# Layer 3's loop: the Exp of a step in two parts, and the values of a step gathered one step ahead

## The chip, the core and the metric

The kernel runs on one core of a Trainium2 chip. The core has five engines that work in parallel, each on its own queue of instructions: TensorE (PE, matrix products into PSUM), VectorE (DVE), ScalarE (ACT), GpSimd (POOL) and SyncE (SP). DMA engines move data between HBM and the on-chip memory SBUF; any of several engines can issue a DMA. The metric is the device time of one execution in microseconds; the number that counts is the median of several runs.

## The reference

Four graph layers run one after the other on a graph of N = 2708 nodes with 128 features and a dense 0/1 adjacency matrix A. Only the fourth (layer 3) is touched by the change:

```python
XW = X @ W
s_col = XW @ a[0, :f];  s_row = XW @ a[0, f:]
Z1 = leaky_relu(s_row[:, None] + s_col[None, :], negative_slope=0.01)
den = exp(Z1)
num = A @ den
att = where(num != 0, den / where(num != 0, num, 1.0), 0.0)
H = A @ (att @ XW)
```

Computed as written, `A @ den` would be a product of two N x N matrices. The kernel uses that `den[r, c]` depends on the two scores alone, and that the leaky relu has two straight pieces: for the columns sorted by score, most of a column of `num` is a running sum over the rows in order of their scores, plus a remainder over a few rows close to the place where the piece changes.

## The kernel before, in words

Layers 0 to 2 are streaming products of the adjacency with the features. Layer 3 then has four stages:

1. Ranks. Every node gets its rank by row score and a slot by column score (lines 679 to 1067), which gives tables: `xw_i` (which 128 nodes form step s), `row_i` (which 124 rows of the transposed adjacency a row set q needs) and `pre_i` (which 4 rows of running sums).
2. Running sums (`sums`, line 818), written to HBM as `pre_d`.
3. The loop over NE = 22 steps of 128 columns each (lines 1183 to 1224). This is where the change is.
4. The last product A @ (att @ XW) (line 1287), with the adjacency streamed in once more by SP's DMAs, into buffers that the loop has freed.

**One step s of the loop.** A step has two row sets, q = 2s and 2s + 1. A row set is a 128 x 2708 tile: 124 gathered adjacency rows and 4 rows of running sums. There are four buffers for them, `hT`, `row_b`, `hs`, `yT` (`regained[q % 4]`).

- `fetch_xw(s)` (line 666, issued by POOL): an indirect DMA that gathers the 128 rows of XW that belong to step s, the *values*, into one of four buffers `xw_s[s % 4]`.
- `fetch_step(s + 2)` (line 1156, POOL): four indirect DMAs, in this order: the rows of set 2s + 4 (`gather_rows`), the running sums of set 2s + 3 (`carry`), the rows of set 2s + 5, the running sums of set 2s + 4. A `carry` writes into the same buffer as its `gather_rows` and waits until those rows have landed.
- VectorE: `xw` times a factor (line 1189), the shifted relu into a tile `e` of 128 x 2708 (line 1193, two buffers for `e`), four small operations that split the next weights into a high and a low part (`densities_of`, lines 1175 and 1176).
- TensorE: `num` in six blocks of 512 columns, four matmuls each (line 1206), through two PSUM banks.
- ScalarE: Ln of each block (line 1211) as it is done, which also frees the bank.
- VectorE: three subtractions `e - ln` (line 1214), of 1536, 1024 and 148 columns.
- `halved(2s + 2)` on VectorE and `halved(2s + 3)` on ScalarE (line 1168): the conversion of the row sets of step s + 1 to the type that the matmuls of line 1206 read.
- ScalarE: Exp over the whole of `e` (line 1220): att for these 128 columns.
- TensorE: `spread_values(s - 1)` (line 1147): twelve matmul instructions (line 1150) that multiply the step's values by the `e` of the step before and add to six accumulators. They come after the products of step s, and free the `e` buffer that the relu of step s + 1 writes.

**What sets the order.** A planner places the instructions on each engine's queue and adds the semaphores. Nearly all of the loop is wrapped in `keep_in_program_order`, which holds these instructions of an engine in the order of the source. `fetch_xw` is not wrapped. The branch taken with this input is `exact`: all conditions on `exact` are true. All issues of POOL carry line 647 in the profile, since they go through the helper `gather`; they are told apart by their tiles.

Of the kernel before, what the change touches and what calls it, by code (L numbers as in the profile page):

```python
# [13 lines left out]
AF = mybir.ActivationFunctionType  # L14
# [5 lines left out]
def kernel(  # L20
# [19 lines left out]
    nc = tc.nc  # L40
# [16 lines left out]
    CUT = 3 * 512  # L57
# [35 lines left out]
    def bank():  # L93
        return ps.tile([P, 512], F32, tag="bank", name="bank")
# [69 lines left out]
    NE = T  # L164
# [321 lines left out]
    def rest(exact, stack3):  # L486
# [159 lines left out]
        def gather(out, src, idx):  # L646
            return nc.gpsimd.indirect_dma_start(  # L647
                out=out,
                out_offset=None,
                in_=src,  # L650
                in_offset=bass.IndirectOffsetOnAxis(ap=idx, axis=0),
            )
# [7 lines left out]
        def gather_rows(a, s):  # L660

            m = gather(a, adj_t[:, :], row_i[:, s : s + 1])
            tc.keep_in_program_order(m)
            return a

        def fetch_xw(s):
            gather(xw_s[s % 4], xw_d[:, :], xw_i[:, s : s + 1])
# [465 lines left out]
        def carry(s):  # L1133
            a = regained[s % 4]
            m = gather(a[SUMS[0] : SUMS[-1] + 1 : SUMS[1] - SUMS[0], :], pre_d[:, :], pre_i[: P - CH, s : s + 1])
            tc.keep_in_program_order(m)
            return a
# [9 lines left out]
        def spread_values(s):  # L1147
            xw, e = done.pop(s)
            for b, (lo, hi) in enumerate(E0):
                m = nc.tensor.matmul(accs[b][:, : hi - lo], xw, e[:, lo:hi], start=(s == 0), stop=(s == NE - 1))  # L1150
                tc.keep_in_program_order(m)

        with tc.tile_pool(name="att", bufs=2) as attp:
            terms = {}

            def fetch_step(s):

                for q in (2 * s, 2 * s + 1):
                    if q < NS:
                        gather_rows(regained[q % 4], q)  # L1160
                    if q <= NS:
                        rows_of[q - 1] = carry(q - 1)

            def halved(q):

                a = rows_of.pop(q)
                r = steps.tile([P, N], F32R, tag="rows", name="rows")
                m = nc.scalar.copy(r, a) if q % 2 else nc.vector.tensor_copy(r, a)  # L1168
                tc.keep_in_program_order(m)
                return r  # L1170

            def densities_of(q):
                d_hi = attp.tile([P, P], F32R, tag=f"d_hi{q % 2}", name="d_hi")
                d_lo = attp.tile([P, P], F32R, tag=f"d_lo{q % 2}", name="d_lo")
                tc.keep_in_program_order(nc.vector.tensor_copy(d_hi, dmat[:, q, :]))
                tc.keep_in_program_order(nc.vector.tensor_sub(d_lo, dmat[:, q, :], d_hi))
                return [d_hi, d_lo]

            nc.scalar.preload_act_table_set("natural_log_exp_and_others")
            if exact:  # L1180
                moving = {q: halved(q) for q in range(2)}
                weights = {q: densities_of(q) for q in range(2)}
            for s in range(NE):
                if s >= 3:
                    fetch_xw(s)
                if exact:
                    fetch_step(s + 2)
                xw = xw_s[s % 4]
                tc.keep_in_program_order(nc.vector.tensor_scalar_mul(xw, xw, c_exp[:, s : s + 1]))  # L1189
                e = attp.tile([P, N], F32, tag="e", name="e")  # L1190
                ln = attp.tile([P, N], F32, tag="ln", name="ln", bufs=1)
                tc.keep_in_program_order(
                    nc.vector.tensor_scalar(e, row_a[:, :N], c_rel[:, s : s + 1], 0.0, ALU.add, ALU.max)
                )
                halves = (2 * s, 2 * s + 1)
                if exact:
                    products = [(d, moving[q]) for q in halves for d in weights[q]]
                    if s + 1 < NE:
                        weights = {q + 2: densities_of(q + 2) for q in halves}
                else:  # L1200
                    products = [(dmat[:, q, :], rows_of.pop(q)) for q in halves]
                beg = 0
                for b, (lo, hi) in enumerate(E0):
                    num = bank()
                    for i, (d, a) in enumerate(products):
                        m = nc.tensor.matmul(  # L1206
                            num[:, : hi - lo], d, a[:, lo:hi], start=(i == 0), stop=(i == len(products) - 1)
                        )
                        tc.keep_in_program_order(m)
                    tc.keep_in_program_order(  # L1210
                        nc.scalar.activation(ln[:, lo:hi], num[:, : hi - lo], AF.Ln, bias=tiny)  # L1211
                    )
                    if b in (2, 4, 5):
                        tc.keep_in_program_order(nc.vector.tensor_sub(e[:, beg:hi], e[:, beg:hi], ln[:, beg:hi]))  # L1214
                        beg = hi
                if not exact:
                    fetch_step(s + 2)
                elif s + 1 < NE:
                    moving = {q + 2: halved(q + 2) for q in halves}
                tc.keep_in_program_order(nc.scalar.activation(e, e, AF.Exp))  # L1220
                done[s] = (xw, e)
                if s:
                    spread_values(s - 1)
            spread_values(NE - 1)
# [65 lines left out]
    with tc.If(some_low > 0) as general:  # L1290
        with ExitStack() as s3:
            rest(False, s3)
    with general.Else():
        with ExitStack() as s3:
            rest(True, s3)
# [32 lines left out]
```

## Time and profile before

| | |
|---|---|
| median of three runs | 851.61 us (849.99 to 853.9) |
| the profiled execution's own time | 853.49 us |
| its span in the profile | 851.7 us |
| busy in the span: PE, DVE, ACT, POOL | 729.7, 583.7, 536.1, 189.2 us |
| mean granted TensorE clock | 0.932 |
| the loop of layer 3 | about 533 to 779 us of the span |
| HBM read | 214.12 MB, 256 GB/s over the span |

Times in the profile are microseconds from the span's start. A line of the list of waits reads: waiting engine, tile and line, what it waited for, then the total, how often, and the longest. A line of the timeline reads: start, duration, engine, line, operation, output <- inputs, and in brackets the idle time of the engine just before it with what ended it. In the timeline `DMA_INDIRECT xw<-xw_d,xw_i` is a step's gather of values, `hT<-in_adj_t_dram,row_i` (or `row_b`, `hs`, `yT`) a gather of rows, and `hT<-pre_d,pre_i` a carry. The duration of such an issue is that of the issue on POOL, not of the transfer. "issue" in a bracket means that the engine waited for nothing that the profile shows.

### The profile page before, as it was taken

The page shows a single profiled execution, that of the slowest core. Times are in us where ns is not written, and L with a number is a line of the kernel's source. Part 1 is how long each engine was busy: PE and PEld are TensorE (multiplying, and loading weights), DVE is VectorE, ACT ScalarE, POOL GpSimd, SP SyncE. Part 2 cuts the span into 40 slices and gives each one's busy share as a digit, 9 for nine tenths or more (in the row PEclk, how much of TensorE's full clock was granted, in tenths as well). Part 3 has the DMA queues.
Part 4 walks back from the last instruction along what each step waited for, and adds up shares of the span by engine and source line. Part 5 has one row for each costly group of instructions (what it writes and reads, how often), then busy time and mean ns, then how long its engine had stood idle before and what let it go on. Part 6 is the DMA issues. An engine that isn't in the chain of part 4 may idle for free.

```text
span 851.7 us, 9005 instructions
## 1 busy us (share of the span) xinstructions
PE 729.7 (86%) x3113; PEld 440.8 (52%) x3113; DVE 583.7 (69%) x1112; ACT 536.1 (63%) x595; POOL 189.2 (22%) x161
## 2 busy tenths in 40 slices
PE   3599999995996979978649785798999989989997
PEld 2333333332775858756216531555555555555785
DVE  5499879786824363447988967776666666655854
ACT  3889999995845473437860026678778777767000
POOL 3000000012201010002000113446666666620010
PEclk9899999997897989988879995899999999999999
DMA  9044444723997989975505985677777776785994
GB/s 339 3 148 180 177 164 182 305 78 148 355 393 284 365 330 395 419 294 208 186 0 184 401 333 210 239 282 272 273 257 287 263 279 255 278 306 229 404 427 139
DMA packets 39476, 218.63 MB, mean 257 GB/s; under 512 B 5108, under 2 KB 13999, under 8 KB 25359
## 3 DMA queue, kind: packets, MB, share of 16 engines
q1 hardware_dynamic: 27704, 150.19, 45.6%
q0 software_dynamic: 8624, 65.76, 21.1%
q10 hardware_dynamic: 3090, 1.99, 0.7%
q8 instruction: 27, 0.44, 0.2%
q14 instruction: 31, 0.25, 0.1%
HBM read 214.12 MB, written 3.79 MB: 256 GB/s over the span
## 4 chain that ended last, share of the span: by engine, by line
PE 14%; DMA 12%; DVE 9%; issue 6%; POOL 6%; ACT 5%; SPq 0%; DVEq 0%; POOLq 0%; ACTq 0%
PE acc L1150 4%; PE bank L1206 4%; DMA hs<-in_adj_t_dram 4%; DMA row_b<-pre_d,pre_i 3%; PE acc L835 2%; DMA row_b<-in_adj_t_dram 2%; ACT rows L1168 2%; POOL hT L647 2%; POOL hs L647 1%; DMA yT<-pre_d,pre_i 1%; PE acc L224 1%; POOL row_b L647 1%; ACT row_a L747 1%; DVE rows L1283 1%; DVE bits L744 1%
## 5 line engine op out<-in xcount | busy, mean ns | idle before, releaser
L1206 PE MATMUL bank<-rows,d_hi 128*128 128x512 f32 (+1 forms) x264 | 106.5, 408 | 24.4 <-ACT ln L1211 12.7
L224 PE MATMUL acc<-rows,h_hi 128*128 128x512 f32 (+1 forms) x264 | 106.5, 408 | 10.3 <-ACT rows L529 6.0
L1150 PE MATMUL acc<-e,xw 128*128 128x512 f32 (+1 forms) x264 | 104.3, 545 | 0.0
L1211 ACT ACTIVATE ln<-bank,tiny 128x512 f32<-128x512 f32 x132 | 79.8, 632 | 33.1 <-PE bank L1206 32.9
L1206 PE MATMUL bank<-rows,d_lo 128*128 128x512 f32 (+1 forms) x264 | 98.7, 385 | 0.0
L224 PE MATMUL acc<-rows,h_lo 128*128 128x512 f32 (+1 forms) x264 | 98.0, 388 | 0.2 <-DVE h_lo L506 0.2
L1214 DVE TENSOR_TENSOR e<-e,ln 128x1536 f32<-128x1536 f32 (+2 forms) x66 | 70.0, 1097 | 15.9 <-ACT ln L1211 15.6
L1206 PEld LDWEIGHTS bank<-rows,d_hi 128*128 128x128 f32 x264 | 51.6, 195 | 53.1 <-ACT ln L1211 31.7
L358 DVE SCALAR_TENSOR_TENSOR tau<-tau,e_hi,a 128x1536 f32<-128x1536 f32 (+1 forms) x44 | 70.5, 1623 | 9.7 <-DMA a<-in_adj_dram 5.6
L1150 PEld LDWEIGHTS acc<-e,xw 128*128 128x128 f32 x264 | 48.4, 190 | 52.6 <-issue 52.6
L355 ACT ACTIVATE tau<-row_a,e_neg,e_lo 128x1536 f32<-128x1536 f32 (+1 forms) x44 | 65.7, 1504 | 3.3 <-PE bank L367 3.2
L224 PEld LDWEIGHTS acc<-rows,h_hi 128*128 128x128 f32 x264 | 52.5, 199 | 24.3 <-ACT rows L529 8.3
L367 PE MATMUL bank<-tau,ones_at 128*32 128x512 f32 (+1 forms) x264 | 51.8, 566 | 8.3 <-DVE tau L358 8.3
L224 PEld LDWEIGHTS acc<-rows,h_lo 128*128 128x128 f32 x264 | 52.6, 200 | 11.8 <-issue 1.9
L1220 ACT ACTIVATE e<-e 128x2708 f32<-128x2708 f32 x22 | 54.1, 2461 | 3.3 <-DVE e L1214 3.3
L224 PE MATMUL acc<-yT,hs 128*128 128x512 f32 x132 | 56.1, 563 | 0.0
L224 PE MATMUL acc<-row_b,hs 128*128 128x512 f32 x132 | 55.3, 557 | 0.0
L1206 PEld LDWEIGHTS bank<-rows,d_lo 128*128 128x128 f32 x264 | 51.6, 195 | 7.0
L224 PE MATMUL acc<-rows,y_hi 128*128 128x512 f32 x132 | 49.8, 384 | 3.8 <-DVE rows L1283 1.9
L224 PE MATMUL acc<-rows,y_lo 128*128 128x512 f32 x132 | 48.4, 382 | 0.0
L529 ACT CAST rows<-dflat 128x1536 fp32r<-128x1536 f32 (+1 forms) x26 | 34.2, 1330 | 20.6 <-DMA dflat<-in_adj_dram 11.2
L1189 DVE TENSOR_SCALAR xw<-xw,c_exp 128x128 f32<-128x128 f32 x22 | 6.4, 290 | 58.2 <-DMA xw<-xw_d,xw_i 58.2
(411 smaller groups left out, 1415.4 us busy)
## 6 DMA issues: line engine op xcount, KB each, us to landing
a<-in_adj_dram SPq DMA_DIRECT2D x21, 1354.0 KB
rows<-in_adj_t_dram SPq DMA_DIRECT2D x16, 1354.0 KB
dflat<-in_adj_t_dram SPq DMA_DIRECT2D x9, 768.0 KB
rows<-in_adj_t_dram SPq DMA_DIRECT2D x9, 768.0 KB
dflat<-in_adj_dram SPq DMA_DIRECT2D x9, 768.0 KB
rows<-in_adj_dram SPq DMA_DIRECT2D x9, 768.0 KB
dflat<-in_adj_t_dram SPq DMA_DIRECT2D x5, 1354.0 KB
hs<-in_adj_t_dram SPq DMA_DIRECT2D x5, 1354.0 KB
```

Source lines behind the costliest of these rows:

```text
L224: nc.tensor.matmul(accs[b][:, : hi - lo], w, moving[:, lo - at : hi - at], start=start and i == 0, stop=stop and i == len(parts) - 1,)
L355: nc.scalar.activation(tau[:, :w], row_a[:, h0:h1], AF.Relu, bias=e_neg[:, t : t + 1], scale=e_lo[:, t : t + 1])
L358: nc.vector.scalar_tensor_tensor(tau[:, :w], tau[:, :w], e_hi[:, t : t + 1], a[:, h0:h1], ALU.add, ALU.mult)
L367: nc.tensor.matmul(den[g : g + 32, : hi - lo], ones_at[:, b // GR, :], tau[:, lo - h0 : hi - h0], start=(t == 0 and b < GR), stop=(t == T ...
L529: m = nc.vector.tensor_copy(r, a) if i % 2 and i > 4 else nc.scalar.copy(r, a)
L647: return nc.gpsimd.indirect_dma_start(out=out, out_offset=None, in_=src, in_offset=bass.IndirectOffsetOnAxis(ap=idx, axis=0),)
L835: m = nc.tensor.matmul(accs[b][64 * h : 64 * h + 2 * NC, : hi - lo], w[:r, t, :], a[:r, lo:hi], start=(t == 0 and i == 0), stop=(t == T - ...
L1150: m = nc.tensor.matmul(accs[b][:, : hi - lo], xw, e[:, lo:hi], start=(s == 0), stop=(s == NE - 1))
L1206: m = nc.tensor.matmul(num[:, : hi - lo], d, a[:, lo:hi], start=(i == 0), stop=(i == len(products) - 1))
L1211: nc.scalar.activation(ln[:, lo:hi], num[:, : hi - lo], AF.Ln, bias=tiny)
L1214: tc.keep_in_program_order(nc.vector.tensor_sub(e[:, beg:hi], e[:, beg:hi], ln[:, beg:hi]))
L1220: tc.keep_in_program_order(nc.scalar.activation(e, e, AF.Exp))
```

## The change

In each step, the values of the next step are gathered in place of the step's own: `fetch_xw(s + 1)` for 3 <= s + 1 < 22, at the same place in the source, ahead of `fetch_step`. The call for step 3's values thus stands in step 2, and the last step makes none. And the Exp is made in two parts: columns 0 to 1535 (`CUT` is 3 * 512, which is also where the first subtraction ends) before the two conversions of the next row sets, and the other 1172 columns after them, where the whole Exp was. The work is the same, with one more ScalarE instruction per step.

```diff
             for s in range(NE):
-                if s >= 3:
-                    fetch_xw(s)
+                if 3 <= s + 1 < NE:
+                    fetch_xw(s + 1)
                 if exact:
                     fetch_step(s + 2)
                 xw = xw_s[s % 4]
...
                         beg = hi
+                tc.keep_in_program_order(nc.scalar.activation(e[:, :CUT], e[:, :CUT], AF.Exp))
                 if not exact:
                     fetch_step(s + 2)
                 elif s + 1 < NE:
                     moving = {q + 2: halved(q + 2) for q in halves}
-                tc.keep_in_program_order(nc.scalar.activation(e, e, AF.Exp))
+                tc.keep_in_program_order(nc.scalar.activation(e[:, CUT:], e[:, CUT:], AF.Exp))
                 done[s] = (xw, e)
```

## The prediction

> **What bounds the kernel now.** I read the waits of 560 to 760 us first: the loop of layer 3 runs from 533 to 779 us, some 10.7 us a step.
>
> ```profile
> DVE xw L1189 <- DMA xw<-xw_d,xw_i: 58.2, 17, 7.7
> POOL hs L647 <- DMA hs<-in_adj_t_dram,row_i: 24.2, 9, 4.0
> POOL hT L647 <- DMA hT<-in_adj_t_dram,row_i: 21.4, 9, 2.8
> PE bank L1206 <- ACT ln L1211: 12.2, 14, 1.2
> ACT rows L1168 <- DMA yT<-pre_d,pre_i: 11.6, 9, 2.0
> ```
>
> The largest wait is the one that the change removes: VectorE waits 3.4 us a step for the values `xw`. But it is no proof of a gain; who sets the pace? GpSimd (POOL) waits for none of the other engines here, only for its own gathers. Its timeline for one step (start, duration; the bracket is the idle time before it):
>
> ```profile
> 640.42 0.95 POOL L647 DMA_INDIRECT xw<-xw_d,xw_i  x1 [0.30 <-issue]
> 641.68 0.93 POOL L647 DMA_INDIRECT hT<-in_adj_t_dram,row_i  x1 [0.30 <-issue]
> 642.92 1.92 POOL L647 DMA_INDIRECT yT<-pre_d,pre_i  x1 [0.30 <-issue]
> 645.14 0.95 POOL L647 DMA_INDIRECT row_b<-in_adj_t_dram,row_i  x1 [0.30 <-issue]
> 648.38 2.24 POOL L647 DMA_INDIRECT hT<-pre_d,pre_i  x1 [2.29 <-DMA hT<-in_adj_t_dram,row_i]
> 650.92 0.95 POOL L647 DMA_INDIRECT xw<-xw_d,xw_i  x1 [0.30 <-issue]
> ```
>
> I call the five V (values), A (first row gather), b (carry for the row before), B (second gather), a (carry into A's row, which waits until A has landed). The ring A, landing, a, V, A closes on itself. Sixteen steps give A 0.94, landing 5.94 (5.52 to 6.28) after its record ends, a 2.30, V 0.95 and two gaps of 0.30: **10.73 us**. V to V from 575.86 to 747.83 is 171.97/16 = 10.75. So POOL paces the loop; PE, stalled 0.5 to 1.2 us a step by a late Ln, needs only 9.92 (its products in the step without a stall: 561.42 to 571.34).
>
> Why is a 2.24 here, and b 1.92, when an undisturbed carry takes 0.90? VectorE's rows of the same step:
>
> ```profile
> 642.91 0.29 DVE L1189 TENSOR_SCALAR xw<-xw,c_exp 128x128 f32<-128x128 f32 x1 [2.89 <-DMA xw<-xw_d,xw_i]
> 643.11 1.62 DVE L1193 TENSOR_SCALAR e<-row_a,c_rel 128x2708 f32<-128x2708 f32 x1
> 648.96 1.56 DVE L1168 CAST rows<-hs 128x2708 fp32r<-128x2708 f32 x1
> ```
>
> b ends at 644.84, 0.11 after the relu (643.11 to 644.73); a at 650.62, 0.10 after the conversion. Through all 95 POOL issues of the loop one rule holds within 0.03 us on average: an issue that begins inside such an operation, or inside a subtraction (L1214), goes on when that ends and takes 0.77 more; one that begins up to about 0.3 us before the relu or the conversion is held to its end plus 0.1; with 0.5 us it gets through.
>
> [...]
>
> **The change, part by part.**
>
> *Exp in two.* ACT's conversions of the two widths show the price: 1.47 us at 1536, 1.15 at 1172, together 2.62 for 2.46, +0.16 a step (3.5 us over 22 steps if uncovered). The cover is ACT's wait for the carried row, 0.4 to 2.0 us a step. The first part can start when the Ln's end, 6.1 us after the products begin; it holds ACT for 1.38 and is done at 7.5; the row comes later than that (below). The next Ln starts after 2.35 + 1.08 instead of 2.35 + 2.36 us from the conversion: 1.28 earlier. That ends PE's stall. Alone it gains little, since POOL paces. The first part adds a wait for the first subtraction, over at 5.7, and the conversion and PE's next products stand behind it; uncovered it would cost them its 1.38 a step.
>
> *Values a step ahead.* The same five issues in the same order; V merely carries the next index, and its buffer was free some 11 us before. VectorE's 3.4 us of waiting disappear, but what follows moves too: today the relu falls 2.7 us after V, harmlessly on b, because it waits for V. Afterwards it starts when PE leaves the buffer `e`, and that is on V and A, in the ring; behind V in POOL's queue stand A, b, B and a, and both conversions wait for these.
>
> The new step, in offsets from c, the start of a: ACT's conversion begins 0.36 later (mean of 17), products at c + 2.86. VectorE's conversion H starts 7.30 after the products (573.22 against 565.91, the step without a stall), so c + 10.16. The relu R starts 5.43 + 4.80 after the products: H + 2.93. An a inside H ends at H + 2.33:
>
> ```profile
> 573.22 1.56 DVE L1168 CAST rows<-hT 128x2708 fp32r<-128x2708 f32 x1
> ```
> ```profile
> 573.85 1.70 POOL L647 DMA_INDIRECT hs<-pre_d,pre_i  x1 [3.99 <-DMA hs<-in_adj_t_dram,row_i]
> 575.86 0.95 POOL L647 DMA_INDIRECT xw<-xw_d,xw_i  x1 [0.30 <-PE acc L1150]
> ```
>
> So V starts at H + 2.64, 0.29 before R[...].
> - V held: it ends at R + 1.72, H + 4.65; A from H + 4.95, through R's small followers to H + 5.85; it lands at H + 11.79.
> - V through: A starts at H + 3.89, inside R, and ends 0.77 after it, H + 5.32; it lands at H + 11.26.
>
> The landing is the next a. With u = c − H, the period is 10.16 + u, and the next u is 1.63 − u (held) or 1.10 − u (through): u swings about a mean of 0.82 or 0.55. The period is **10.98** or **10.71**; scatter of 0.3 us in the landings will give both, and I take 10.85, 0.10 over today's. From A(4) to A(19) are 15 periods: +1.5 (−0.6 to +3.4). The gain at a (2.30 becomes some 1.5) is spent at V or A.
>
> *The start.* In step 0 nothing hides the first part: products of step 1 at 544.9 for 543.96. Step 3 gets a V that it hadn't (the fourth values were fetched before the loop): its A starts near 566.8, in the relu, ends near 568.9 for 566.08 and lands at 574.8 for 573.85; A(4) ends near 579.4 for 578.06: **+1.4** (0 to 2).
>
> *The end.* Step 20's values are issued at 747.83, when the last layer's loads begin, and land 7.3 us later:
>
> ```profile
> 755.13 0.29 DVE L1189 TENSOR_SCALAR xw<-xw,c_exp 128x128 f32<-128x128 f32 x1 [7.70 <-DMA xw<-xw_d,xw_i]
> ```
> ```profile
> 762.54 0.76 PE L1206 MATMUL bank<-rows,d_hi 128*128 128x512 f32 x1 [3.40 <-DVE rows L1168]
> ```
>
> Relu, subtractions and conversion follow late, PE stands idle and then runs its products at a lower clock (0.63 for 0.40 us each), 6.88 us to the next spread. Afterwards those values are there; ACT's conversion (756.40, still late behind the loads) sets the start, 758.9; the products take 5.5. Spread at 764.4 for 769.42: **−5.0** (−3.6 to −5.5). Step 21's values land near 755 and are needed near 758. The last product's loads wait for buffers that this loop frees (from 778.80), so the end moves with the loop.
>
> **Sum:** +1.4 + 1.5 − 5.0 = −2.1. On the profiled execution's 853.49 (span 851.7) that is 851.4; on the runs' median 851.61, 1.9 below the profiled one, it is **849.5**. About 0.5%, 4.3 us, is what a measurement of this kernel can tell from no change.
>
> **Rivals.**
> 1. *POOL gets free.* If a slips past the subtractions, or landings come at 5.5 us, the ring falls below PE's 9.95: 15 × 0.80 = 12 less, and the end's 5: about 836; in part of the steps, 843. For it: POOL issues undisturbed would cost 9.4 a step. Against it: a earlier than H falls into the subtractions, and is held all the same.
> 2. *The relu ahead of V (the slower side).* If R starts a few tenths earlier than H + 2.64, V waits for all of it, ends at R + 2.39, A at R + 3.65: landing at H + 12.25, u's mean 1.05, period 11.21. 15 × 0.46 = 6.9, + 1.4 − 5.0 = +3.3: 854.9; with landings at their slowest, 6.28 (half of the 0.34 counts), or only half of the end's gain, 857.5. It decides from R − V below zero, 0.3 us from my figure; over 0.5% it needs a period of 11.28.
> 3. *The change doesn't do as it says.* `fetch_xw` isn't pinned, and the planner could leave V where it was. Then only the split works: PE's stall goes, a meets less of H, period some 10.4, no gain at the end: 846.5. Against it: V lies in program order in every step from the fourth.
>
> **How the numbers follow.** Forecast 0.50 (its own range 846.5 to 853), rival 1 0.15, rival 2 0.30, rival 3 0.05. Faster by over 0.5% (below 847.3): rival 1, half of rival 3, a fifth of the forecast: 0.27. Slower (above 855.9): half of rival 2 and a fifth of the forecast[...]: 0.25. The rest, 0.48, within. Range 842.5 to 857.5: it leaves out rival 1's lower half and the tails.
>
> **What would show it.** Right: no wait of DVE for `xw` after 560 us; the relu at a spread's end, within 0.5 us of V; V or A about 1.7 us, a about 1.5; V to V about 10.85; PE idle some 0.9 a step, now for `rows`; step 21's products without the 3.4 us. Wrong: a period near 10 with PE busy through, or above 11.2 with V over 2 us. Most fragile is the 0.29 us between V and R.

## The result, and the profile after

| | before | after |
|---|---|---|
| median of 20 runs each | 851.79 us | 856.17 us (849.29 to 864.18) |
| ratio, 95% interval | | 1.0037 [1.0015, 1.0058] |
| profiled execution's own time, span | 853.49, 851.7 us | 857.27, 855.5 us |
| A to A in the loop, mean of 15 periods | 10.76 us | 10.96 us |

The change makes the kernel some 0.4% slower. The whole interval lies above 1, although the size is about the 0.5% that I had called the limit of this measurement. The medians lie 4.4 us apart (0.5%); the ratio, which leaves out one slow run of the changed kernel (864.18 us), is a little smaller. I had forecast 2 us less, and it became more: inside the range, but slower where I had forecast faster.

The waits of the kernel after, 560 to 760 us, a selection (engine, tile and line, what it waited for: total, times, longest):

```profile
DVE e L1214 <- ACT ln L1211: 43.2, 38, 4.7
POOL hs L647 <- DMA hs<-in_adj_t_dram,row_i: 22.4, 8, 4.5
DVE e L1193 <- PE acc L1150: 20.8, 18, 1.2
POOL hT L647 <- DMA hT<-in_adj_t_dram,row_i: 20.4, 9, 3.4
PE bank L1206 <- ACT rows L1168: 10.7, 14, 2.1
POOL yT L647 <- DMA yT<-in_adj_t_dram,row_i: 4.8, 3, 3.5
POOL row_b L647 <- DMA row_b<-in_adj_t_dram,row_i: 4.1, 3, 1.8
```

VectorE's 58.2 us of waiting for `xw` are gone, but its waiting as a whole is not: the subtractions now wait 43.2 us for the Ln (6.4 before) and the relu 20.8 us for the spread to leave `e` (1.2 before), 64 us together. PE waits 10.7 us for the rows where it had waited 12.2 us for a late Ln. POOL's own two waits for A are nearly as long as before (42.8 for 45.6). The last two lines are POOL's *other* carry, b, which now waits for B; before there was one such wait, of 1.5 us. Here is the step that the prediction showed, on POOL and on VectorE:

```profile
639.98 2.03 POOL L647 DMA_INDIRECT xw<-xw_d,xw_i  x1 [0.30 <-issue]
642.31 1.00 POOL L647 DMA_INDIRECT hT<-in_adj_t_dram,row_i  x1 [0.30 <-DVE d_hi L1175]
643.61 0.89 POOL L647 DMA_INDIRECT yT<-pre_d,pre_i  x1 [0.30 <-issue]
644.80 2.28 POOL L647 DMA_INDIRECT row_b<-in_adj_t_dram,row_i  x1 [0.30 <-ACT ln L1211]
649.26 0.90 POOL L647 DMA_INDIRECT hT<-pre_d,pre_i  x1 [2.18 <-DMA hT<-in_adj_t_dram,row_i]
```
```profile
640.25 1.63 DVE L1193 TENSOR_SCALAR e<-row_a,c_rel 128x2708 f32<-128x2708 f32 x1 [1.15 <-PE acc L1150]
644.50 1.76 DVE L1214 TENSOR_TENSOR e<-e,ln 128x1536 f32<-128x1536 f32 x1 [1.68 <-ACT ln L1211]
```

The relu starts 0.27 after V, and V takes 2.03 for 0.95: it is held to the relu's end (641.88) plus 0.13. A, b and a get through in 0.9 to 1.0. B begins 0.30 after the subtraction has begun (644.50 to 646.26) and takes 2.28, which is the subtraction's end plus 0.82. So in this step the hold has moved from b and a to V and B.

The means of the 16 steps from A(4) to A(19), with the two gaps of 0.30 in each ring sum (b and B are not in the ring):

```
         V     A     landing  a     ring sum   measured   b     B
before   0.95  0.94  5.94     2.30  10.73      10.76      1.66  1.21
after    1.87  1.06  6.22     1.25  11.00      10.96      1.17  1.78
```

And the end of the loop. Of before, the last B of the loop, B(19), and the carry b(20) that goes into its rows:

```profile
740.95 1.88 POOL L647 DMA_INDIRECT yT<-in_adj_t_dram,row_i  x1 [0.30 <-ACT ln L1211]
749.10 0.90 POOL L647 DMA_INDIRECT yT<-pre_d,pre_i  x1 [0.31 <-issue]
```

Of after, the same two, the first load of the last product between them, and what follows from the carry:

```profile
744.60 2.31 POOL L647 DMA_INDIRECT yT<-in_adj_t_dram,row_i  x1 [0.30 <-ACT ln L1211]
...
749.32 0.36 SPq L69 DMA_DIRECT2D hT<-in_adj_t_dram  x1
...
755.87 1.71 POOL L647 DMA_INDIRECT yT<-pre_d,pre_i  x1 [3.54 <-DMA yT<-in_adj_t_dram,row_i]
...
763.41 2.45 ACT L1168 CAST rows<-yT 128x2708 fp32r<-128x2708 f32 x1 [4.76 <-DMA yT<-pre_d,pre_i]
...
765.91 0.79 PE L1206 MATMUL bank<-rows,d_hi 128*128 128x512 f32 x1 [4.18 <-ACT rows L1168]
```

Before, b(20) did not wait for data; after, it waits 3.54 for B(19) and can start only 8.96 us after B's record ends. ACT's conversion, 756.40 in the kernel before, comes at 763.41. PE waits 4.18 for it, where it had waited 3.40 for VectorE's late rows. The spread that follows begins at 773.28 for 769.42.

The ledger of the two profiled executions, in us: the loop begins 1.2 earlier (upstream of the change); A(4) ends 0.7 later, counted from there; from A(4)'s end to A(19)'s end 165.59 for 161.38, +4.2 (1.3 of it because A(19) itself is held, 2.21 for 0.94); from A(19)'s end to the end of the span 112.39 for 112.26, +0.1. The sum is +3.8, the difference of the spans.

### The profile page after: what moved, and what is told of

Same layout as the page of the kernel before. It is cut to its first block, busy times and chain, and to the rows that moved or that the text cites. A ratio compares the mean times of both kernels' runs of the same rounds, so it can differ in the third digit from the quotient of the medians.

```text
span 855.5 us, 9024 instructions
## 1 busy us (share of the span) xinstructions
PE 736.1 (86%) x3113; PEld 440.2 (51%) x3113; DVE 585.4 (68%) x1112; ACT 540.0 (63%) x617; POOL 195.8 (23%) x161
## 4 chain that ended last, share of the span: by engine, by line
PE 22%; DMA 13%; DVE 11%; ACT 4%; issue 2%; POOL 1%; SPq 0%; DVEq 0%; ACTq 0%; POOLq 0%
PE bank L1206 9%; PE acc L1150 7%; DMA yT<-pre_d,pre_i 4%; DMA hs<-in_adj_t_dram 4%; ACT rows L1168 3%; PE acc L224 2%; DMA row_b<-in_adj_t_dram 2%; DMA row_b<-pre_d,pre_i 1%; DMA yT<-in_adj_t_dram,row_i 1%; DVE e L1193 1%; DVE bits L744 1%; PE acc L835 1%; DVE rows L1286 1%; ACT row_a L747 1%; DVE row_b L864 1%
## 5 line engine op out<-in xcount | busy, mean ns | idle before, releaser
L1206 PE MATMUL bank<-rows,d_hi 128*128 128x512 f32 (+1 forms) x264 | 109.7, 420 | 23.2 <-ACT rows L1168 14.9
L1211 ACT ACTIVATE ln<-bank,tiny 128x512 f32<-128x512 f32 x132 | 81.6, 635 | 33.5 <-PE bank L1206 31.8
L647 POOL DMA_INDIRECT xw<-xw_d,xw_i x22 | 36.9, 1678 | 92.2 <-PE acc L835 85.8
L1193 DVE TENSOR_SCALAR e<-row_a,c_rel 128x2708 f32<-128x2708 f32 x22 | 35.9, 1634 | 23.2 <-PE acc L1150 23.2
```

The source lines that it names most:

```text
L647: return nc.gpsimd.indirect_dma_start(out=out, out_offset=None, in_=src, in_offset=bass.IndirectOffsetOnAxis(ap=idx, axis=0),)
L1206: m = nc.tensor.matmul(num[:, : hi - lo], d, a[:, lo:hi], start=(i == 0), stop=(i == len(products) - 1))
```

## The experiments

The theory after the result: (1) the loop pays at V, which the relu now holds, and gains it back at a only in part, with b's new waits on top; (2) at the end, the values are no longer late, but the last rows are, since B(19) lands among the last product's first loads (the *flood*). Rivals: the loss comes from one part of the change alone, or B(19) is late because the subtraction held its issue. All ratios are to runs of the kernel before on the same chip, whose median lay between 853.21 and 853.98 there; so the ratios are compared, not the times.

### The same kernel once more (e1)

No edit.

> The changed kernel once more. [...]again about 0.4% over before (855 us), a values gather to values gather of 10.9 to 11.1 us in the loop, the values or the first row gather held by the relu in nearly every step. Theory of the loop's end (the gain of 5 us forecast there is lost because step 19's second row gather lands about 9 us after its issue, among the last product's loads): the times fall into two groups some 5 us apart, near 851 and near 857, by whether the last carry waits for that gather; a profile near 857 shows that wait (3 to 4 us on POOL near 752 us), one near 851 doesn't. If the end plays no part, the times form one group.

857.58 us (851.84 to 862.69, 22 runs), ratio 1.0047 [1.0025, 1.0068]. Its profile has the same marks: V 1.89, b held up by B in 7 places, b(20) among them, period 11.06. At the end b(20) waits 3.34 and PE 4.72, and from A(19)'s end to the end of the span it is 112.0 us (112.39 in the first profile). The two groups of times that were expected are not there: the single times scatter over 11 us without separate levels, and those of the kernel before over 10 (848.68 to 858.96), so the times don't bear out that part of the theory, though the profile shows the wait at the end again.

### The Exp in two parts alone (e2)

Against the changed kernel:

```diff
-                if 3 <= s + 1 < NE:
-                    fetch_xw(s + 1)
+                if s >= 3:
+                    fetch_xw(s)
```

> Only the Exp in two parts; the values gathered in their own step as before. [...]the Ln of the next step starts 1.28 us earlier, TensorE's stall of 0.5 to 1.2 us goes, VectorE's conversion comes some 0.7 us earlier against the carry, which then is held less: period 10.3 to 10.5 us for 10.75, about 5 us less than before, 846 to 848; TensorE's wait of 3.4 us in the last step stays. Rival, that the split is what costs (0.16 us more of ScalarE per step, conversion and next products pushed back): 22 x 0.16 = 3.5 more, about 855.

850.43 us, ratio 0.9967 [0.9952, 0.9982]: the split alone gains 0.3%. The period is 10.50, as expected for a faster PE that makes a meet less of VectorE's conversion: V 1.02, A 0.94, landing 5.99, a 1.98, together 10.53. The median is 2 us above the expected 846 to 848; the profile is that of the fastest of the 22 runs (845.89). The wait for `xw` is nearly as large as ever in this faster kernel, 560 to 760 us:

```profile
DVE xw L1189 <- DMA xw<-xw_d,xw_i: 57.4, 17, 6.5
```

So that wait was slack, and the change gives this gain away with its other part.

### The values a step ahead alone (e3)

Against the changed kernel:

```diff
-                tc.keep_in_program_order(nc.scalar.activation(e[:, :CUT], e[:, :CUT], AF.Exp))
...
-                tc.keep_in_program_order(nc.scalar.activation(e[:, CUT:], e[:, CUT:], AF.Exp))
+                tc.keep_in_program_order(nc.scalar.activation(e, e, AF.Exp))
```

> Only the values a step ahead; the Exp whole, where it was. [...]the relu leaves the harmless place on the carry and falls on the values or the first row gather, and VectorE's conversion stays late (TensorE's stall is still there), so the period is 11.3 to 11.65 us: 8 to 13 us more in the loop, 0 to 5 less at its end: 856 to 865, slower than the full change. Rival, that VectorE's wait of 3.4 us per step was a cost: faster than before, 846 or less.

864.25 us (6 runs), ratio 1.0135 [1.0095, 1.0176], period 11.53: as expected. V 1.66, A 1.35, landing 6.09 and a 1.75 make 11.45 with the two gaps. V and a are both held, often in the same step: a 2.01 from 619.02 and V 2.02 from 621.34.

No b waits in these steps, and B takes 1.03 on average: it begins ahead of the subtraction. At the end B(19) takes 0.94, and b(20) doesn't wait:

```profile
761.53 0.94 POOL L647 DMA_INDIRECT yT<-pre_d,pre_i  x1 [0.31 <-issue]
```

From A(19)'s end to the end of the span it is 108.4 us, for 112.26 before, though the last product's loads come as early as there (the first 4.7 us after B(19)'s record in both). So at the end early values do gain, 3.8 us; in the loop they cost more than that. On the whole they cost about 1.3%; with the split beside them, some two thirds of it is repaired.

### The relu twice (e5)

If the relu holds POOL's issues, it is in POOL's ring, although VectorE has 1.7 us to spare in front of the subtraction.

```diff
+                tc.keep_in_program_order(
+                    nc.vector.tensor_scalar(e, row_a[:, :N], c_rel[:, s : s + 1], 0.0, ALU.add, ALU.max)
+                )
```

> The relu of layer 3's steps (L1193) is executed twice in place, which leaves its result as it is. [...]a step's relu begins within 0.3 us of V and of A, so a second relu of 1.6 us holds V or A, which are in the ring, for up to 1.6 us more; part of that is given back at a, whose conversion comes later. V and A together 1 to 1.6 us longer than the 2.9 of the changed kernel, the ring's period +0.5 to +0.8 over its 10.96 (11.5 to 11.8), the time 7 to 12 us more: 864 to 869. Rival: VectorE is not in the ring, it stands idle 1.7 us before the first subtraction, waiting for the Ln: the second relu goes into that idle time, period 10.9 to 11.1 and time 855 to 859.

868.66 us (4 runs), ratio 1.0144 [1.0097, 1.019], period 11.60: as expected. The first relu holds V, the second holds A (in 10 of the 16 steps):

```profile
648.04 2.02 POOL L647 DMA_INDIRECT xw<-xw_d,xw_i  x1 [0.30 <-issue]
648.32 1.63 DVE L1193 TENSOR_SCALAR e<-row_a,c_rel 128x2708 f32<-128x2708 f32 x1 [1.15 <-PE acc L1150]
649.99 1.63 DVE L1196 TENSOR_SCALAR e<-row_a,c_rel 128x2708 f32<-128x2708 f32 x1
650.37 2.06 POOL L647 DMA_INDIRECT hT<-in_adj_t_dram,row_i  x1 [0.30 <-issue]
```

V and A take 3.74 together for 2.93, 0.8 more (1 to 1.6 had been expected; a is as short as it was, and the landing gives 0.2 back, 5.99 for 6.22). In the step shown V ends 0.11 after the first relu (649.95) and A 0.81 after the second (651.62), so the second holds an issue of POOL as the first does; what in the chip makes the hold the traces don't show. VectorE itself still has room: it waits 23.7 us for the Ln between 560 and 760 us. So here VectorE work that fits into VectorE's waiting costs 0.64 us a step through POOL (11.60 for 10.96).

### The values a step ahead, but behind A (e4)

```diff
-            gather(xw_s[s % 4], xw_d[:, :], xw_i[:, s : s + 1])
+            return gather(xw_s[s % 4], xw_d[:, :], xw_i[:, s : s + 1])
...
-            def fetch_step(s):
+            def fetch_step(s, between=None):
...
                         gather_rows(regained[q % 4], q)
+                    if q == 2 * s and between is not None:
+                        tc.keep_in_program_order(fetch_xw(between))
...
-                if 3 <= s + 1 < NE:
-                    fetch_xw(s + 1)
+                ahead = s + 1 if 3 <= s + 1 < NE else None
                 if exact:
-                    fetch_step(s + 2)
+                    fetch_step(s + 2, ahead)
+                elif ahead is not None:
+                    fetch_xw(ahead)
```

V is also pinned in its place here, which it was not in the changed kernel; its place there was the same in every step all the same.

> The full change, but with the values gather issued after the first row gather of a step and not ahead of it, so that its 0.95 us and its hold by the relu fall into the time in which POOL waits for those rows anyway. [...]the ring loses the values gather: period 10.0 to 10.4 us, TensorE's bound being 9.95: 5 to 11 us less than before in the loop, 0 to 5 less at the end: 838 to 849. Rival, that the ring of POOL isn't the pace and the loss comes from elsewhere (ScalarE, the end): as the full change, 854 to 857.

847.09 us (11 runs), ratio 0.9918 [0.9885, 0.9951]; period 10.46 where 10.0 to 10.4 had been expected. The relu now holds A, and V runs in A's landing time, outside the ring:

```profile
639.26 2.02 POOL L647 DMA_INDIRECT hT<-in_adj_t_dram,row_i  x1 [0.30 <-issue]
641.58 1.01 POOL L647 DMA_INDIRECT xw<-xw_d,xw_i  x1 [0.30 <-PE bank L1209]
...
644.09 1.69 POOL L647 DMA_INDIRECT row_b<-in_adj_t_dram,row_i  x1 [0.30 <-issue]
647.66 1.21 POOL L647 DMA_INDIRECT hT<-pre_d,pre_i  x1 [1.88 <-DMA hT<-in_adj_t_dram,row_i]
```

A 1.90, from A's end to a 6.76, a 1.46 and one gap of 0.30 make 10.42. One issue out of the ring takes half a microsecond off each step. B is held here too (1.94), and b waits in 7 places, the longest b(20) with 3.06.

### The last product's loads later (e6, e8, e7)

To take the flood away without touching the loop, the first loads take first the buffers that the loop frees last (order `hs`, `yT`, `dflat`, `hT`, `row_b`) and are held in that order on SP's queue. The same edit was made on three kernels: the changed one (e6), the split alone (e8, the control) and the values behind A (e7).

```diff
-    def fill(a, src, t):
+    def fill(a, src, t, pin=False):
...
-        nc.sync.dma_start(a[: rows(t), :], src[t * P : t * P + rows(t), :])
+        m = nc.sync.dma_start(a[: rows(t), :], src[t * P : t * P + rows(t), :])
+        if pin:
+            tc.keep_in_program_order(m)
...
-            spare = [*regained, dflat[:, NPAD : NPAD + N], None]
+            spare = [regained[2], regained[3], dflat[:, NPAD : NPAD + N], regained[0], regained[1], None]
...
-                    fill(a, adj_t, t)
+                    fill(a, adj_t, t, exact)
```

> The last product's first loads take the buffers that come free latest first and stay in that order, so that none of them starts before about 758 us; nothing in the loop is changed. Flood theory: the gather B(19) landed 9.0 us late because it shared the DMA engines with those loads. Here it lands about 6 us after its record, b(20) starts near 753 without a wait of 3.5, ACT's conversion of the last row comes near 760, and the spread of the last step 3 to 5 us earlier; the time 851 to 853.5, if the later loads are still there when the last product needs them. Rival: B(19) was late because the subtraction held its issue (2.31 for 0.95) and not for the loads: b(20) still waits 2 to 3.5 us and the time stays at 856 to 858, or above that by late loads.

852.92 us (851.67 to 858.37, 14 runs), ratio 0.9995 [0.9975, 1.0014] for the 1.0037 and 1.0047 with the loads as they were. The loop is the same (10.94). Its end (line numbers are two higher; the first load starts at 761.28):

```profile
745.64 2.30 POOL L649 DMA_INDIRECT yT<-in_adj_t_dram,row_i  x1 [0.30 <-ACT ln L1213]
...
754.55 0.89 POOL L649 DMA_INDIRECT yT<-pre_d,pre_i  x1 [1.19 <-DMA yT<-in_adj_t_dram,row_i]
759.83 2.45 ACT L1170 CAST rows<-yT 128x2708 fp32r<-128x2708 f32 x1
```

B(19) is held as long as in the changed kernel (2.30 for 2.31), and b(20) can start 6.61 us after its record for 8.96. That decides for the flood: the hold makes B late, but the 2.4 us more of landing come from the loads. ACT's conversion no longer waits, and PE's gap is gone; the spread that follows begins at 767.75 for 773.28. What the core did between 756 and 772 us, in two stretches (busy time and count of PE, weight loads, DVE, ACT, POOL; then PE's clock, DMA share, GB/s), of after and of this kernel:

```profile
756.00:764.00 8.00, 5.73 (x20) 2.90 (x18) 5.58 (x6) 2.93 (x4) 1.58 (x1) 1.00 1.00 394
764.00:772.00 8.00, 6.09 (x15) 4.80 (x16) 0.70 (x1) 5.00 (x5) 0.00 (x0) 0.57 0.80 316
```
```profile
756.00:764.00 8.00, 8.00 (x30) 4.79 (x29) 6.28 (x6) 7.17 (x8) 0.00 (x0) 1.00 0.22 65
764.00:772.00 8.00, 8.00 (x28) 4.54 (x27) 3.44 (x4) 5.75 (x8) 0.00 (x0) 1.00 1.01 425
```

With the flood the DMA engines are full (1.00) while PE stands, and PE's clock is 0.57 on average in the stretch in which it comes back; without it they are at 0.22 and PE is busy through. From A(19)'s end to the end of the span it is 106.96 us, for 112.39 after and 112.26 before. In the changed kernel, from 748 to 752 us POOL's queue takes 86% of the 16 engines' time and SP's 1%, from 752 to 756 us, in which B(19)'s last rows land, POOL's takes 18% and SP's 84%. With the loads late (the first at 761.28) the engines are at 0.69 from 747 to 756 us, for 0.95 in the changed kernel.

> The kernel before with the Exp in two parts alone, with the late loads: the control for what late loads do by themselves. In that kernel b(20) does not wait, but step 20's values, issued in the flood, land 7 us after their issue, and PE stands 3.0 us for them. Flood theory: these land 1 to 2 us earlier, 847 to 850 for the 850.4 of the split alone. If late loads cost by themselves at the last product: 851 to 854, and by as much the other two runs are to be corrected.

845.92 us (6 runs), ratio 0.9902 [0.9868, 0.9935], where the split alone had 0.9967 [0.9952, 0.9982]: better than expected. That b(20) does not wait in the split alone was wrong: it waits 1.57 there, and not here. In the split alone, with early loads, VectorE waited 6.49 for step 20's values and PE then 3.00; here it waits 2.96 and PE's gap is gone. From A(19)'s end to the end it is 108.1, for 110.6 with the early loads. So the late loads are worth 2.5 us by themselves at this place, in a kernel whose values come late, and 5.4 in the changed one (single profiles; the two of the changed kernel differ by 0.4 here). With the loads away, and beside the split, early values are worth only 1.1 us at the end (106.96 for 108.1). In the loop they cost 0.38 a step there (10.94 for 10.56).

> The kernel with the values' gather issued behind the first row gather, with the late loads as well. Flood theory: its b(20) waited 3.06 us too, and loses that wait: 842 to 845 where the same kernel with early loads had 847.1. Rival (no part of the end comes from the loads): 846 to 848. If late loads cost by themselves: over 848.

845.22 us (842.04 to 846.5, 6 runs), ratio 0.9893 [0.9864, 0.9923]; its interval overlaps that of the same kernel with early loads, so a gain here is not shown. In its profile b(20) still waits 2.36, until 745.18, well ahead of the first load at 749.74: that wait isn't the loads' doing, and the expectation that it goes failed. Nor did the loads do much with V behind A when they came early: b(20) could start 6.75 us after B(19)'s record there (at 746.47) and 6.03 here, for 8.96 in the changed kernel; why is not shown. It is the fastest kernel of the study, but it can't be told from the split with late loads, which leaves V where it was.

### The values behind both gathers (e9, e10)

If held row gathers are what makes b wait, then V should take the subtraction's hold in B's place (order A, b, B, V, a); e10 adds the late loads. Against the kernel with V behind A:

```diff
-                    if q == 2 * s and between is not None:
+                    if q == 2 * s + 1 and between is not None:
```

> The changed kernel with V, a step ahead, issued behind both row gathers (order A, b, B, V, a); loads as in the changed kernel. Theory (an issue of a row gather that is held lands late, and the carry behind it waits): VectorE's relu holds A, as in the kernel with V behind A alone, and then B comes 1.3 us earlier and begins ahead of the subtraction, which V now takes: B back from 1.9 to 1.0-1.3 us, V about 2, b's waits of 0.6 to 1.8 us gone from the loop, the period 10.46 to 10.0-10.3, B(19) landed before the flood, and 840 to 846 for the 847.1 of V behind A. Rival: b waits because landings are long, whatever is held; then b's waits stay, the period stays at 10.4 to 10.5 and the time at 846 to 849.

> The same with the last product's loads late. Theory: as B(19) lands before the loads even without this, little is left for it, 0 to 2 us less than the run above: 839 to 845. Rival (b's waits stay): 3 us less than the run above, as with V behind A: 843 to 846.

849.64 us (15 runs), ratio 0.9967 [0.9948, 0.9986], and 848.43 (15 runs), ratio 0.9948 [0.993, 0.9966], which overlap; periods 10.69 and 10.64. Both expectations failed, and the one behind them: V is too late here. VectorE waits for it in every step again, and with it the relu moves, off A and onto b:

```profile
638.10 1.84 POOL L647 DMA_INDIRECT xw<-xw_d,xw_i  x1 [0.30 <-issue]
...
643.45 1.96 POOL L647 DMA_INDIRECT yT<-pre_d,pre_i  x1 [1.04 <-DMA yT<-in_adj_t_dram,row_i]
```
```profile
643.49 0.28 DVE L1192 TENSOR_SCALAR xw<-xw,c_exp 128x128 f32<-128x128 f32 x1 [3.67 <-DMA xw<-xw_d,xw_i]
```

In this step V's record ends at 639.94 and VectorE gets the values at 643.49, 3.55 us later; in the kernel before it was 1.54 (641.37 to 642.91). b waits for B in nearly every step, though B takes no longer than in the changed kernel (1.47 for 1.78). So a hold of B is not the only thing that makes b wait; how much of it is B's hold and how much the crowding of the transfers stays open.

## Why the prediction was wrong, point by point

- **The end, −5.0: failed.** This is the step that turned the sign; +0.1 was measured. I followed the values through the flood and took for granted that the carry's rows would come as before ("ACT's conversion (756.40, still late behind the loads) sets the start, 758.9"). But B(19) ends 4.1 us later than before (746.91 for 742.83; 3.7 of it is the ring, since A(19) ends at 743.11 for 739.44, the rest B's own hold), and the first load comes 2.4 us after it, where it came 4.7 after (747.51 before). The gain that I had named exists: with early values alone (e3), where B(19) is not held and the first load comes 4.7 us after it, the end takes 3.8 us less (108.4 for 112.26). In the changed kernel B's late rows take it back in whole. With the loads out of the way its end takes 5.3 us less than before (106.96 for 112.26); that this is the size of the forecast is luck, since early values make only 1.1 of it there.
- **The ring, +1.5: the mechanism right, the size too small; +4.2 was measured.** V was to start 0.29 before the relu: it starts 0.27 to 0.29 before it in 10 of the 16 steps from 585 us on. I mixed "held" (10.98) and "through" (10.71) evenly; V is held in 14 of the 16. That 10.96 is nearly the held value is in part luck: two terms that I had not moved so moved against each other. The landing grew by 0.28. It is 6.00 on average over the 12 steps in which b doesn't wait and 6.87 in the 4 in which it does, so b's waits make 0.22 of the 0.28: B and a stand behind b in POOL's queue. As b was outside the ring, I costed it and B at nothing, and did not follow the subtraction onto B. The hold at a was mis-sized the other way, 1.25 for some 1.5. From A(4)'s end to A(19)'s end +4.2 came for +1.5: 3.0 are the period's 0.20 in 15 steps, the rest is A(19), which is held at the end of the count.
- **The start, +1.4:** +0.7, inside its bounds.
- **The Exp in two:** the parts take 1.49 and 1.18, +0.21 for the whole's 2.46, where +0.16 was worked out. PE's 12.2 us of waits for a late Ln ended as said. "Alone it gains little, since POOL paces" was half wrong: it gains 0.3% in the runs. As rival 3 had it, an earlier PE lets a meet less of VectorE's conversion (a 1.98 for 2.30).
- **Rival 1** (POOL gets free) did not happen. **Rival 2** gave the nearest time (854.9, with half of the end's gain 857.5), but not by its mechanism: the relu doesn't come ahead of V, the period is 10.96 and not 11.21, and the end's gain is lost in whole. **Rival 3** (V left in place) did not happen either; as an experiment it had about the period it was given (10.50 for 10.4), and gained 3.4 us on its own runs of before where the rival had 5.1.

## What to carry to other kernels

A wait removed from an engine that doesn't set the pace moves that engine's work, and the moved work can hold the engine that does (here the relu held V, 1.87 us for 0.95): before moving it, list what it will overlap with there, also the issues that are off the ring. In a ring of issues on one queue, take an issue out of the ring (behind the one whose landing is awaited, as V behind A, with a period of 10.46 us for 10.96) rather than make it earlier in place, but not so far back that its data come late (10.69 with V behind both gathers). Where the next stage's loads start as soon as buffers come free, check what is still to land for this stage (here B(19)'s rows, for which b(20) could start 8.96 us after the record among the loads and 6.61 without them); taking first the buffers that are freed last was worth 0.4 to 0.7% in two of four kernels (the changed one and the split alone) and showed no clear gain in the other two.

## What the runs showed of the hardware

- The carry behind a gather of 124 rows could start 6.61 us after the gather's record without SP's loads, and 8.96 among them, with the same hold of the gather's issue (2.30 and 2.31).
- In the kernel after, 12 of POOL's issues began inside a subtraction of 1536 columns, 0.06 to 0.81 us after its start, and ended 0.76 to 0.82 us after its end. Four second gathers that began 0.03 to 0.33 us ahead of one took 0.95, unheld. The relu is otherwise: 13 V's that began 0.06 to 0.29 us ahead of it were held to its end plus 0.12. So a few tenths of a microsecond decide whether B is held at all.
- Around PE's stall of 4.18 us (761.73 to 765.91) the granted clock was 1.00 from 762 to 764.7 us and 0.50 from 764.8 to 771.5; in the kernel without the stall it was 1.00 from 756 to 772. The products after the stall took 7.4 us to the next spread (765.91 to 773.28), for 6.0 in the split alone (755.86 to 761.85), where the clock stayed at 1.00 from 756 to 764: in the changed kernel 1.4 us came on top of the stall's own length. The length alone doesn't tell what follows: in the kernel before, the products behind a stall of 3.40 us ran at a clock of 0.50 (762.5 to 764 us) and took 0.63 us each from the second on; with V behind A those behind one of 2.10 us also took 0.63 (756.48 to 759.47); in the split alone those behind one of 3.00 us took 0.39 to 0.50.
- Doubling a VectorE operation that had room on VectorE lengthened the step by 0.64 us (11.60 for 10.96), with V and A, the issues of GpSimd's DMAs in the ring, 0.8 longer together (3.74 for 2.93).
